# Regrouping SyncE's loads in a fused graph-attention and hypergraph kernel: adjacency ahead of the store, blocks behind the sums' read

## The chip, the cores and the metric

The kernel runs on one core of a Trainium2 chip. The metric is device time in microseconds (us) of one execution; the number quoted for the kernel before is the median of three runs. The profile is one further execution, recorded by the hardware profiler, with a time of its own.

## The reference

The input is a batch of 128 graphs, each with 128 nodes of 512 features (`x`) and a 128 x 128 adjacency (`adj`). Two layers follow each other, both with a residual and a layer norm. Cut to what matters:

```python
# layer 0: graph attention, 8 heads of 64
feats = einsum('bnf,hfu->bhnu', X, W)
dense = leaky_relu(e_self[..., :, None] + e_neigh[..., None, :], 0.2)
att   = softmax(dense - 1e10 * (1 - A), -1)
x = layernorm(x + relu(att @ feats + b))
# layer 1: hypergraph convolution twice, H = (adj != 0), w = first row of adj
conv(x, W) = Dn * (H @ (Be * (H.T @ (x @ W.T)))) + b     # Dn = 1/(H @ w), Be = 1/column sums of H
h = layer_norm(relu(conv(x, W1)))        # 512 -> 1024
x = layernorm(x + (conv(h, W2) + x))     # 1024 -> 512
```

All of it is in float32.

## The kernel before

Two graphs are one **pair**; there are 64 pairs, and everything is done a pair at a time with the 128 nodes on the 128 partitions. The pairs are pipelined: while one pair has its features made, the one before it is in its attention, the one before that in the hidden layer, and a fourth in its output. Matrix products on TensorE (PE) use a scheme with seven half-size products instead of eight, whose sums are made by GpSimd (POOL), whose intermediate copies are made by ScalarE (ACT), and whose last additions are made by VectorE (DVE).

The order of all work is written out by hand. Each step has a due time inside a period of `T = 38.6` units and a lag in periods; the list `todo` is sorted by that time, and the instructions of each engine are issued in the sorted order. The units are those of the schedule, not of the chip. What is due early stands early in its engine's queue, and each engine runs its queue in order. So a due time of a load sets nothing but its place in SyncE's (SP) queue.

SP issues nearly all DMAs, and no other work. In one period it issues, by due time within the period (numbers are line numbers of the profile):

- at 6.2 `e_write` (623): the exponentials of the first half (`nb`) are written to DRAM as `ed`; at 10.0 `e_read` (631) reads them back in four DMAs as `eb`, so that DVE can transpose them blockwise into `eT` (640); at 10.9 and 14.9 the same for the second half;
- at 17.0 `write_nodes` (374): the scales of the nodes, made by DVE in `nodes` (360 to 369) from the adjacency `a` and its first row `w`;
- at 19.5 `store` (1043): the output of a pair that is done;
- at 20.5 `load_edges` (137): the adjacency once more in blocks of 32 x 32, `ab`, in four DMAs, which DVE transposes in `edges` (421);
- at 25.0 `spread_rows` (552), the write of one small tile as `rd`; at 27.0 `neighbours` (570), which reads it back as `nb` for all partitions, 512 KB twice; these are the neighbours' part of the scores. POOL adds the mask to them (589), ACT applies the leaky activation (605) and, in the next period, the exponential (619);
- at 28.0 `spread_nodes` (576, `dnb`); at 28.92 `write_sums` (962, `sd`); at 31.0 `load_rows` (120, `x`); at 31.5 `read_sums` (967, `sums_out`);
- at 0 of the next period `load`: the adjacency `a` (106) and its first row for all partitions, `w` (112), two DMAs;
- at 2.0 `load_blocks` (129): the features in blocks of 32 rows, `xb`, in four DMAs, which DVE transposes in `x_transpose` (385) as input of the feature products.

The tiles of `a` and `w` have two buffers; `xb` and `ab` have one each, so that the load for a pair waits until DVE has transposed the blocks of the pair before. In the program's instruction list, each DMA of SP also waits on the completion of the eighth DMA before it, since eight completion semaphores are used in turn.

ACT's queue matters too: the copies of the propagated features, `zT` (831), which the next hidden products on PE wait for, stand behind the leaky activations of two quarters of the scores.

The last pairs have due times of their own, and so has the start (the dictionary `first`); pairs 0 and 1 load in another order.

Of the kernel before, what the change touches and what calls it, by code (L numbers as in the profile page):

```python
# [20 lines left out]
def kernel(  # L21
# [1102 lines left out]
    for t, fn, *args in (  # L1124
# [14 lines left out]
    T = 38.6  # L1139
    todo = [  # L1140
        (11.1, prepare_first, (0,)), (12.0, prepare_first, (1,)), (15.45, prepare_first_sums, ()),
        (12.1, load_weights, (nc.scalar, w2_blocks, w2t, DH // 2, QU)),
        (13.05, prepare_vectors, ()),
        (14.05, load_weights, (nc.scalar, w1_blocks[:2], w1t, F // 2, HALF)),
        (12.95, load_first_row, (1,)),
        (15.46, load_weights, (nc.sync, w1_blocks[:1:-1], w1t, F // 2, HALF)),
        (16.1, everywhere, (b2_bc, b2, nc.sync)),
        (79.0, prepare_hidden, (nc.gpsimd, 0)), (79.1, prepare_hidden, (nc.gpsimd, 1)),
# [54 lines left out]
        todo.append((time, run, (fn, p, args)))  # L1203
    for p in range(PAIRS):
        if p > 1:
            todo.append(({2: 79.5, 3: 143.1}.get(p, p * T), load, (p,)))
            todo.append((16.2 if p == 2 else p * T + (19.0 if p == 3 else 2.0), load_blocks, (p,)))
            todo.append((p * T + (28.5 if p == 2 else 20.5), load_edges, (p,)))
        for lag, time, name, pairs, fn, args in steps:
            if p not in pairs:  # L1210
                continue
            if p == 0 and lag == 2 and time < 8.5:
                time *= 0.2
            if p == LAST:

                time = {
                    ("attend", 0): 24.25, ("attended", 0): 25.5,
                    ("attend", 1): 25.95, ("attended", 1): 26.0,
                    ("residual", 1): 26.3, ("rstds", "a"): 26.4,
                }.get((name,) + args[:1], time)  # L1220
            if p == LAST - 1:
                time = {
                    ("product", 2): 24.22 if (lag, time) > (3, 20.0) else time,
                    ("product", 5): 29.5 if (lag, time) > (3, 20.0) else time,
                    ("squares", 0): 26.5, ("squares", 1): 26.6, ("h_sums", 2): 22.3,
                    ("h_rstd",): 4.6, ("y_scale", 1): 5.8, ("y_scale", 0): 5.9,
                }.get((name,) + args[:1], time)
            time += (p + lag) * T
            todo.append((
                first.get((name, p) + args, first.get((name, p), time)), run, (fn, p, args)  # L1230
            ))
# [46 lines left out]
```

## Time and profile before

| what | value |
|---|---|
| time, median of 3 runs | 2394.72 us (2393.39 to 2398.32) |
| the profiled execution's own time | 2398.11 us |
| its span, first to last instruction | 2396.3 us |
| TensorE (PE) matmul busy | 2361.6 us, 99% |
| VectorE (DVE) busy | 2087.9 us, 87% |
| GpSimd (POOL) busy | 1823.2 us, 76% |
| ScalarE (ACT) busy | 1528.2 us, 64% |
| SP's DMA queue, share of 16 DMA engines | 50.1% |
| moved | 347.09 MB, mean 145 GB/s |
| granted TensorE clock | 0.997 |

Landing times, median from issue to landing: `nb` 6.0 us for 512 KB, `ed` 3.6 us for 512 KB, `eb` 2.9 us for 128 KB, `x` 4.5 us for 512 KB, the store 2.9 us for 512 KB, `xb` 5.5 us for 128 KB, `a` 2.3 us for 128 KB, `w` 5.1 us for 64 KB, `dnb` 7.8 us for 128 KB, `ab` 2.5 us for 32 KB.

How to read it: a busy time is the time in which an engine had an instruction of its own at work, and PE's is near the whole span. DMA-issuing instructions are not counted as busy; the time in SP's rows is the time that SP needs to issue, and the landing is given apart. The chain of waits is followed back from the end of the program, at each step to what released an instruction or to the one before it on its engine.

### The profile page before, as it was taken

The page shows a single profiled execution, that of the slowest core. Times are in us where ns is not written, and L with a number is a line of the kernel's source. Part 1 is how long each engine was busy: PE and PEld are TensorE (multiplying, and loading weights), DVE is VectorE, ACT ScalarE, POOL GpSimd, SP SyncE. Part 2 cuts the span into 40 slices and gives each one's busy share as a digit, 9 for nine tenths or more (in the row PEclk, how much of TensorE's full clock was granted, in tenths as well). Part 3 has the DMA queues.
Part 4 walks back from the last instruction along what each step waited for, and adds up shares of the span by engine and source line. Part 5 has one row for each costly group of instructions (what it writes and reads, how often), then busy time and mean ns, then how long its engine had stood idle before and what let it go on. Part 6 is the DMA issues. An engine that isn't in the chain of part 4 may idle for free.

```text
span 2396.3 us, 80729 instructions
## 1 busy us (share of the span) xinstructions
PE 2361.6 (99%) x32309; PEld 1898.1 (79%) x32309; DVE 2087.9 (87%) x4456; ACT 1528.2 (64%) x4481; POOL 1823.2 (76%) x2060
## 2 busy tenths in 40 slices
PE   7999999999999999999999999999999999999998
PEld 6777777778778878778778788788888888788886
DVE  7988888888898898898888888988988988988875
ACT  4565765756667667667667566676676675676672
POOL 5877777777777877877877778778778778778774
PEclk9999999999999999999999999999999999999999
DMA  6555555555555555555555555555555555555541
GB/s 197 133 145 153 144 138 142 151 145 148 143 148 147 153 146 150 145 145 153 146 144 156 142 148 151 150 146 146 148 146 152 147 149 141 149 151 144 147 129 37
DMA packets 431134, 347.09 MB, mean 145 GB/s; under 512 B 151440, under 2 KB 380328, under 8 KB 430760
## 3 DMA queue, kind: packets, MB, share of 16 engines
q1 hardware_dynamic: 427288, 337.46, 50.1%
q8 instruction: 256, 4.19, 0.8%
q10 hardware_dynamic: 3472, 4.47, 0.6%
q14 instruction: 118, 0.97, 0.2%
HBM read 239.08 MB, written 102.73 MB: 143 GB/s over the span
## 4 chain that ended last, share of the span: by engine, by line
PE 81%; DMA 8%; DVE 4%; ACT 3%; POOL 2%; SPq 1%; issue 1%; DVEq 0%; POOLq 0%; ACTq 0%
PE phX L97 16%; PE pyX L97 15%; PE pfX L97 8%; PE phW L97 8%; PE pyW L97 7%; PE phY L97 4%; PE pfW L97 4%; PE pav L705 4%; PE pq L97 4%; PE pz L97 4%; PE pyY L97 4%; DMA ed<-nb 3%; DMA nb<-rd 2%; PE pfY L97 2%; ACT nb L605 1%; DMA rd<-rows 1%
## 5 line engine op out<-in xcount | busy, mean ns | idle before, releaser
L344 ACT COPY py<-pyX 128x257 f32<-128x257 f32 x189 | 70.6, 374 | 535.4 <-PE pyX L97 441.2
L97 PEld LDWEIGHTS phX<-zS,w_sb 128*64 128x64 f32 x6144 | 346.2, 137 | 37.8 <-POOL ft L744 23.4
L97 PE MATMUL phX<-zS,w_sb 128*64 128x128 f32 x6144 | 369.0, 273 | 2.6 <-ACT ph L344 2.6
L906 POOL TENSOR_TENSOR sq<-sq 128x512 f32<-128x512 f32 (+2 forms) x384 | 343.1, 894 | 20.1
L589 POOL TENSOR_TENSOR nb<-nb,neg 128x512 f32<-128x512 f32 x256 | 319.7, 1283 | 38.1 <-DMA nb<-rd 22.8
L605 ACT ACTIVATE nb<-nb,ft 128x128 f32<-128x128 f32 x1020 | 325.4, 392 | 21.8 <-POOL nb L589 21.7
L619 ACT ACTIVATE nb<-nb,nm 128x128 f32<-128x128 f32 x1024 | 319.2, 391 | 4.3 <-DVE nm L611 4.0
L769 POOL TENSOR_TENSOR rso<-veo,mhalf 128x2 f32<-128x2 f32 x63 | 44.1, 700 | 337.9 <-DVE veo L767 337.9
L97 PE MATMUL pyX<-w_sb,hS 128*64 128x257 f32 x2016 | 242.4, 381 | 0.0
L883 ACT ACTIVATE h<-h,vecs 128x128 f32<-128x128 f32 x768 | 240.5, 393 | 2.4 <-DVE h L868 1.4
L97 PE MATMUL pyX<-w_sb,h 128*64 128x257 f32 x2016 | 240.8, 379 | 0.5 <-ACT py L344 0.5
L97 PE MATMUL pyW<-w_sb,hS 128*64 128x256 f32 x2016 | 240.3, 379 | 0.1
L611 DVE TENSOR_REDUCE nm<-nb 128x4 f32<-128x512 f32 x256 | 175.3, 685 | 54.9 <-ACT nb L605 50.5
L744 POOL TENSOR_TENSOR ft<-ft,b_bc 128x512 f32<-128x512 f32 x128 | 203.9, 1613 | 6.2 <-ACT ft L533 6.2
L97 PEld LDWEIGHTS pyX<-w_sb,h 128*64 128x64 f32 x2016 | 149.8, 137 | 70.0 <-ACT py L344 0.9
L97 PEld LDWEIGHTS pyW<-w_sb,hS 128*64 128x64 f32 x2016 | 149.8, 137 | 69.2 <-issue 0.7
L97 PEld LDWEIGHTS pyX<-w_sb,hS 128*64 128x64 f32 x2016 | 144.7, 137 | 60.9
L640 DVE STREAM_TRANSPOSE eT<-eb 128x512 f32<-128x512 f32 x252 | 163.7, 686 | 12.0 <-DMA eb<-ed 11.1
L807 DVE SCALAR_TENSOR_TENSOR o<-y,b_bc 128x512 f32<-128x512 f32 x128 | 166.2, 1337 | 0.0
L1008 DVE SCALAR_TENSOR_TENSOR y<-y,rsh,bw_bc 128x512 f32<-128x512 f32 x126 | 150.2, 1230 | 16.3 <-POOL rsh L1004 16.3
L894 ACT ACTIVATE sq<-h 128x512 f32<-128x512 f32 x256 | 160.8, 629 | 2.1
L469 POOL TENSOR_TENSOR hS<-h 128x512 f32<-128x512 f32 x126 | 161.9, 1285 | 0.0
(178 smaller groups left out, 5568.1 us busy)
## 6 DMA issues: line engine op xcount, KB each, us to landing
nb<-rd SPq DMA_DIRECT2D x127, 512.0 KB, 6.0
ed<-nb SPq DMA_DIRECT2D x126, 512.0 KB, 3.6
eb<-ed SPq DMA_DIRECT2D x504, 128.0 KB, 2.9
x<-in_x_dram SPq DMA_DIRECT2D x64, 512.0 KB, 4.5
out_dram<-o SPq DMA_DIRECT2D x63, 512.0 KB, 2.9
xb<-in_x_dram SPq DMA_DIRECT2D x248, 128.0 KB, 5.5
a<-in_adj_dram SPq DMA_DIRECT2D x64, 128.0 KB, 2.3
w<-in_adj_dram SPq DMA_DIRECT2D x128, 64.0 KB, 5.1
```

Of the source, the lines that this page charges most:

```text
L97: nc.tensor.matmul(to[rows], lhs[:, rows], rhs, start=start, stop=stop, skip_group_check=True)
L469: engine.tensor_tensor(t[:, i], in0, in1, op=op)
L589: nc.gpsimd.tensor_tensor(t, t, neg[:, :, None, :].to_broadcast([P, NB, HH, B]), op=ALU.add)
L605: nc.scalar.activation(t, t, AF.Prelu, bias=s["ft"][:, g, h, 0:1], alpha=SLOPE)
L611: nc.vector.tensor_reduce(s["nm"][:, g, hs], scores(p, s, g, hs).rearrange("p b h j -> p h b j"), AX.XY, ALU.max, negate=True,)
L619: nc.scalar.activation(t, t, AF.Exp, bias=s["nm"][:, g, h:h + 1])
L640: nc.vector.transpose(s["eT"][:, g, hs, :].rearrange("p h (b i) -> p h b i", b=NB), s["eb", g][:, :, hs, :].rearrange("p b h j -> p h b j"),)
L744: nc.gpsimd.tensor_tensor(t, t, b0_bc.rearrange("p (h u) -> p h u", h=H), op=ALU.add)
L807: nc.vector.scalar_tensor_tensor(s["o"][:, g, :], s["y"][:, g, :], 2.0, b2_bc, op0=ALU.mult, op1=ALU.add)
L883: nc.scalar.activation(dst[:, k, :], src[:, k, :], AF.Relu, bias=b1_sb[:, c:c + 1])
L894: nc.scalar.activation(s["sq"][:, g, q * KH // 2:(q + 1) * KH // 2, :], hid(s, g, q), AF.Square, scale=DH ** -0.5,)
L906: nc.gpsimd.tensor_tensor(t[:, :n, :], t[:, :n, :], t[:, n:2 * n, :], op=ALU.add)
```

## The change

Three due times are changed, for pairs from 5 on. Pairs 2, 3 and 4 keep theirs, now written as numbers.

```diff
     for p in range(PAIRS):
         if p > 1:
-            todo.append(({2: 79.5, 3: 143.1}.get(p, p * T), load, (p,)))
-            todo.append((16.2 if p == 2 else p * T + (19.0 if p == 3 else 2.0), load_blocks, (p,)))
-            todo.append((p * T + (28.5 if p == 2 else 20.5), load_edges, (p,)))
+            todo.append(({2: 79.5, 3: 143.1, 4: 154.4}.get(p, p * T - 21.5), load, (p,)))
+            todo.append(({2: 16.2, 3: 134.8, 4: 156.4}.get(p, p * T - 3.5), load_blocks, (p,)))
+            todo.append(({2: 105.7, 3: 136.3, 4: 174.9}.get(p, p * T - 2.8), load_edges, (p,)))
```

Within a period, SP's queue becomes, with the moved loads marked: `ed`, `eb`, `ed`, `eb`, `dd` (374), **`a`, `w` of the next pair**, store, `rd`, `nb`, `dnb`, `sd`, `x`, `sums_out`, **`xb`, `ab` of the next pair**. Before, it was: `ed`, `eb`, `ed`, `eb`, `dd`, store, **`ab` of this pair**, `rd`, `nb`, `dnb`, `sd`, `x`, `sums_out`, **`a`, `w`, `xb` of the next pair**. So `a` and `w` are issued 21.5 units earlier, `xb` 5.5 and `ab` 23.3 units earlier than before. The queues of the other engines keep their order, and the bytes moved are the same.

## The prediction

> **What bounds the kernel now.** I read the page's busy times first: TensorE (PE) is busy 2361.6 us of a 2396.3 us span, so all that any change of loads can win is inside the 34.7 us that are left, and most of those lie in the first 140 us and in the last pair. To see where the rest lies I took the start of the residual addition at line 807, which comes once a pair, as a clock: 44 pairs in a row, from 657.10 to 2257.69, follow each other at 36.37 us almost without exception; the 14 pairs before, from 138.68, do not. The busy times of these two stretches:
>
> ```profile
> 138.68:657.10 518.42, 512.42 (x7060) 405.62 (x7058) 451.84 (x967) 333.30 (x981) 396.05 (x449) 1.00 0.52 145
> 657.10:2257.69 1600.59, 1600.48 (x22180) 1294.47 (x22178) 1420.09 (x3037) 1048.11 (x3081) 1249.89 (x1409) 1.00 0.53 148
> ```
>
> The columns are the stretch, its length, and the busy time of PE, weight loads, VectorE (DVE), ScalarE (ACT) and GpSimd (POOL), then clock, DMA share and GB/s. In the second stretch PE is never idle: 1600.59 / 44 = 36.38 us a pair is PE's own time, and no load can shorten it. In the first, 518.42 / 14 = 37.03 us: 14 x 36.38 = 509.3, so 9.1 us are lost there, and they are the whole prize. Later pairs add 0.4 us of it.
>
> PE's waits in the first stretch name the place:
>
> ```profile
> PE phX L97 <- ACT zT L831: 4.7, 7, 1.5
> ```
>
> (A few more end with the transposed attention matrix eT.) ACT is late with zT because its queue holds the leaky activations of the next scores before it. What those wait for is in the chain of waits through this stretch, which PE leaves altogether for two pairs (start, length, what):
>
> ```profile
> 356.50 6.30 DMA ed<-nb
> ...
> 364.67 4.74 DMA ed<-nb
> ...
> 371.01 3.21 DMA eb<-ed
> ...
> 376.33 2.61 DMA rd<-rows
> 378.96 4.69 DMA nb<-rd
> ...
> 393.46 6.66 DMA ed<-nb
> ```
>
> The reader is to see a loop of transfers: exponentials of one half written to DRAM (`ed`, 6.3 us) and read back transposed, the other half likewise, then the small write `rd`, the broadcast `nb`, scores, and again `ed`. It is 393.46 - 356.50 = 36.96 us long, 0.6 more than PE's pair. In these pairs the loop, not PE, sets the time. In the chain of a later pair (1639.9 to 1676) there is nothing but PE.
>
> SyncE's (SP) own order of issues, one pair of the slow stretch, shows what stands next to the two transfers of the loop that can be moved by the change:
>
> ```profile
> 484.51 0.40 SPq L1043 DMA_DIRECT2D out_dram<-o  x1
> 484.96 2.47 SPq L137 DMA_DIRECT2D ab<-in_adj_dram  x4
> 487.53 0.40 SPq L552 DMA_DIRECT2D rd<-rows  x1
> 490.88 0.94 SPq L570 DMA_DIRECT2D nb<-rd  x2
> ...
> 500.51 0.44 SPq L106 DMA_DIRECT2D a<-in_adj_dram  x1
> 500.99 1.39 SPq L112 DMA_DIRECT2D w<-in_adj_dram  x2
> 502.49 1.85 SPq L129 DMA_DIRECT2D xb<-in_x_dram  x4
> 505.71 0.34 SPq L623 DMA_DIRECT2D ed<-nb  x1
> 511.16 1.26 SPq L631 DMA_DIRECT2D eb<-ed  x3
> ```
>
> `nb` is issued as soon as `rd` has landed, `eb` as soon as `ed` has. So `rd` took 3.35 us here, behind the store and four `ab`; in a later pair the same order gives 1654.49 to 1655.99, 1.50 us. And `ed` took 5.45 us, behind `a`, `w`, `xb`; a later pair has 1672.35 to 1674.98, 2.63 us. What flowed meanwhile:
>
> ```profile
> 501.00:505.00 4.00, 3.83 (x72) 3.78 (x72) 2.11 (x5) 4.00 (x14) 3.89 (x8) 1.00 0.21 58
> 505.00:509.00 4.00, 4.00 (x78) 4.00 (x76) 3.52 (x4) 2.92 (x11) 3.78 (x5) 1.00 0.81 251
> ```
>
> While `a` and `w` are at the head (501 to 505) the DMA engines are busy for 0.21 and move 58 GB/s; `xb` and `ed` then crowd into the next four at 251 GB/s. `w` is the row that is read for 128 partitions; the page gives it 5.1 us to land for 64 KB. It holds up what follows.
>
> **What the skill says.** The Trainium skill, DMA: Bandwidth & Descriptors, section "Queues, rings and completion order": each DMA engine consumes one queue's descriptors in ring order. All of SP's transfers are one queue, so a transfer inherits what is ahead of it; 3.35 against 1.50 us for the same 16 KB agrees. The same page, "Why small descriptors are slow (HBM only)": each packet has a fixed overhead. The trace agrees in kind: an `ab` block of 32 KB lands in 2.5 us (median), `a` of 128 KB in 2.3. Perfetto Trace Analysis, "DMA Instruction — HWDGE (DVE, Sync)": SP's time for a DMA does not hold the movement of data; here 0.34 us for `ed` against 2.63 to 5.45 until it has landed. So I count SP's issue time and the landing apart.
>
> **The change, part by part**, per pair from pair 5 on. Nothing is added or removed; eleven DMAs (one `a`, two `w`, four `xb`, four `ab`) change places.
>
> `a` and `w` leave the place ahead of `xb` and go behind the write of the node scales, ahead of the store, a period earlier. At the old place SP gets 500.51 to 502.49 back: 2.0 us. At the new place it spends 0.44 + 1.39 = 1.8 us after 482.73, where in the slow pair it waited for the store's data until 484.51, 1.8 us: hidden, to within some tenths. In later pairs that gap is 1647.33 to 1651.44, 4.1 us. If the cover is gone the store is late, which nothing waits for but its buffer, one period on. Buffers of `a` and `w` are two deep; their last readers, the mask and the node scales two pairs back, are over half a period done, so no wait. The slow `w` now drains ahead of store and `rd`: two `w` issued by 484.6 land 5.1 us later, 489.7, and `rd` must follow.
>
> `ab` leaves the place between store and `rd`: 2.47 us of SP, four transfers of 128-byte runs. `rd` is issued when its rows are ready (SP was late by 0.1 us at most), so the issue wins nothing; the landing does. Bounds for `rd`: it becomes 1.5 us (gain 1.9), or is held by `w` until 489.7 + 0.7 = 490.4 (gain 0.5). I take 1.0.
>
> `xb` moves up by the 2.0 us; `ab` comes behind it, ahead of `ed`. SP: 500.51 + 1.85 + 2.47 + gaps = 505.0, against 505.71 when `ed`'s exponentials are ready: hidden by 0.7 us; beyond it each us of SP delays `ed`, both reads of `eb` and the second `ed` queued behind it. New wait: `ab` has one buffer, so its first block waits for DVE's transpose of the old one (line 421). In the pair at 1200 that ends at 1227.67, and SP gets there after 1232; in a slow one (423.42) it is 3 us ahead too: nothing. Besides, every SP DMA waits for the landing of the eighth before it: `ed` now waits for the first `xb`, 500.5 + 5.5 (median landing) = 506.0, up to 0.3 us late; with `w` gone from its front `xb` should land sooner. Bounds for `ed`: the same load ahead of it and no gain, 0.3 lost; or nothing ahead, 2.63 us, 2.8 gained. With `xb` 2 us earlier and 128 KB of small runs in place of 256 KB with the slow row I take 1.5 gained.
>
> Sum on the loop: -1.0 - 1.5 = -2.5 us (bounds -0.5 + 0.3 = -0.2 to -4.7) against 0.65 needed to get from 37.03 under 36.38. PE binds from then on; what is won beyond that is slack. At the switch pair 5's `a`, `w` still meet pair 4's `ab` ahead of one `rd` (SP's issues at 113.5 to 117.6): up to 1 us once. The loop wins 1.8 us a pair on PE, so some two pairs are needed to catch up: 0.5 to 1 us lost. So 1.7 us of the 9.1 stay, 7.4 go: 2398.11 (the profiled execution; its span is 2396.3) - 7.4 = 2390.7. It was 3.4 us above the median of the runs, 2394.72. PE's part being fixed, I read that as 3.4 us fewer lost in the loop: the median run loses some 9.1 - 3.4 = 5.7 and its floor is 2398.11 - 9.1 = 2389.0, or 2388.6 with the later 0.4. Of 5.7 I leave 1.2: 2390.2 us.
>
> **The rivals.**
>
> *Nothing to see.* The slow stretch ends at 657 by chance (after one PE wait of 1.5 us the loop ran uncongested), and `ab` and `w` only change places as obstacles: -0.2 on the loop. Then the runs spread as before, 2393 to 2397. For it: the bytes per pair are the same. Against: both transfers sit in the chain of waits by name, and 58 GB/s is no saturated engine.
>
> *Slower: `ed` is gated.* Place: SP between the sums' read and the write of `ed`. `ab` behind `xb` takes more than the 0.7 us of cover (one `xb` issue took up to 2.3 us, one `w` 2.0), or the first `xb` lands late. In fast pairs `ed` can land some 2.5 us later before DVE waits (last read of `eb` issued to its transpose 5.5 us, landing 2.9); from there the loop binds in all pairs. At the price of the slow stretch, 0.65 us, 44 more pairs are 29 us: 2423; a third of them gives 2404. For it: in pairs 7 to 9 `ed` takes 5.8 to 6.7 us, eT is late by up to 2.0 and PE by 0.5. Against: the work that is taken from ahead of `ed` is slower than what is put there.
>
> *More than forecast.* The loop is short at once and also the unevenness from 100 to 138 (about 1 us over PE's time) goes: 2388.
>
> **How the numbers follow.** Forecast 0.57, with its own range 2388.8 to 2392; more than forecast 0.10; nothing 0.20; slower 0.13. The line of 0.2%, which is about what a measurement of this kernel can tell from no change, is 4.8 us: 2389.9 and 2399.5. The forecast lies across the first: 0.34 of its 0.57 below, 0.23 above; with the 0.10, faster 0.44. Same is 0.23 + 0.19 = 0.42 (0.01 of the "nothing" case goes to slower), slower 0.14. The range leaves out the slower rival and a thin tail below: 2387.8 to 2398.
>
> **What would show it.** The lines of the loop leave the chain of waits after some 250 us, and PE's wait for zT falls from 4.7 us to under 1.5 in the stretch from 138 to 657. `rd` to `nb` is 1.5 to 2.5 us there, `ed` to `eb` 3 to 4.5. SP's store follows `w` with no long wait. The pair stays 36.37 us later on. Wrong it would be if `ed` goes out well behind its exponentials (SP's wait on ACT for line 623 gone) or lands after over 5 us in the later pairs, or if `rd` behind `w` takes 3 us still.

## The result

The changed kernel takes 2392.21 us (median of 18 runs, 2390.08 to 2394.99) against 2396.05 us of the kernel before on the same chip (18 runs, 2393.39 to 2398.49). The ratio is 0.9985, with a 95% interval of 0.9978 to 0.9991. So a gain of 3.8 us, or 0.15%, is there, inside the 0.2% that was named as the line. In a second set, on another chip, the same kernel had a ratio of 0.9989 (0.9982 to 0.9995).

The profiled execution took 2392.25 us, with a span of 2390.5. The same two stretches as for the kernel before, cut by the start of the residual addition at line 807, in the profile of the changed kernel (stretch, length, busy time of PE, weight loads, VectorE, ScalarE and GpSimd, clock, DMA share, GB/s):

```profile
139.16:652.59 513.43, 510.98 (x7060) 406.16 (x7058) 451.28 (x967) 333.75 (x981) 397.91 (x449) 1.00 0.51 147
689.72:2253.78 1564.06, 1564.06 (x21677) 1313.18 (x21675) 1389.55 (x2969) 1024.68 (x3011) 1222.31 (x1377) 1.00 0.52 148
```

The second stretch holds 43 pairs: 1564.06 / 43 = 36.37 us, PE's own time as before. The first holds 14 pairs and is 513.43 - 14 x 36.37 = 4.25 us too long, where the kernel before lost 9.24 us counted in the same way. PE's waits in this first stretch, after:

```profile
PE phX L97 <- ACT zT L831: 2.1, 4, 1.0
```

4.7 us in seven waits have become 2.1 us in four. The chain of waits of the changed kernel, in the same place as the one shown of before, where it leaves PE (start, length, what):

```profile
373.60 0.25 DVE rows L542
...
373.87 3.49 DMA rd<-rows
...
377.80 8.89 DMA nb<-rd
```

`ed` and `eb` are gone from it. What is left is the branch `rd`, `nb`, mask. SP's queue in one pair of the first stretch:

```profile
478.01 0.43 SPq L106 DMA_DIRECT2D a<-in_adj_dram  x1
478.49 0.94 SPq L112 DMA_DIRECT2D w<-in_adj_dram  x2
480.86 0.40 SPq L1043 DMA_DIRECT2D out_dram<-o  x1
483.93 0.33 SPq L552 DMA_DIRECT2D rd<-rows  x1
486.90 0.92 SPq L570 DMA_DIRECT2D nb<-rd  x2
...
496.81 1.86 SPq L129 DMA_DIRECT2D xb<-in_x_dram  x4
498.77 1.88 SPq L137 DMA_DIRECT2D ab<-in_adj_dram  x4
501.96 0.35 SPq L623 DMA_DIRECT2D ed<-nb  x1
506.63 1.73 SPq L631 DMA_DIRECT2D eb<-ed  x4
```

The order is the one that the change describes. `ed` takes 506.63 - 501.96 = 4.67 us here. But `rd`, with no `ab` ahead of it any more, but `a`, `w` and the store, still takes 2.97 us. That second fact was not forecast, and it is what most of the experiments came to be about.

Four figures from the traces serve from here on. Pairs are counted by the clock at line 807; the `rd` that is issued in a pair's interval belongs to the pair two further on. "ed" is the time from the issue of the first of a pair's two writes `ed` to that of its first read, and "rd" from its issue to that of `nb` (medians). "mask" is the start of POOL's mask (line 589) after the pair's clock at line 807 (mean). "loss" is what the pairs take over 36.37 us. Worked out from the traces, in us:

```
            pairs 2 to 15                  pairs 17 to 59
            ed     rd     mask    loss     ed     rd     mask    loss
before      5.83   2.82   24.48   9.2      3.47   1.52   22.98   0.3
after       4.53   2.99   23.89   4.2      2.69   1.43   22.88   0.1
```

The mask tells most of the loss. In 57 of the pairs 1 to 59 of the kernel before, and in 57 of them in the changed one, a pair is longer than 36.37 us by just what its mask starts later than 23.91 us (to within 0.06 us), and no longer where it starts earlier. Summed over the first 14 pairs the mask is late by 9.0 us before and by 3.5 after; the other 0.8 us after lie in pairs 8 and 9, and their cause was not followed. Of the 0.59 us by which the mask came earlier, 0.49 are that `rd` goes out earlier (on average 15.54 us after the clock before, 15.05 after): with `ed` back sooner, the rows are ready in time. The time of `rd` itself gave nothing (2.85 and 2.87 on average), `nb` 0.12.

The kernel before had two kinds of slow pairs. In pairs 2, 3, 7, 8 and 9 `rd` went out late (15.5 to 16.8 us), so the loop was closed; they lost 4.1 us. In pairs 4, 5, 6, 10, 11, 12 and 15 it went out at 15.1 to 15.2 us, so the loop was open, and the slow `rd` itself made the mask late; they lost 5.1 us.

### The profile page after: what moved, and what is told of

Its sections match the earlier page's. It is cut to its first block, busy times and chain, and to the rows that moved or that the text cites. A ratio compares the mean times of both kernels' runs of the same rounds, so it can differ in the third digit from the quotient of the medians.

```text
span 2390.5 us, 80668 instructions
## 1 busy us (share of the span) xinstructions
PE 2357.9 (99%) x32309; PEld 1947.1 (81%) x32309; DVE 2089.6 (87%) x4456; ACT 1529.1 (64%) x4481; POOL 1826.4 (76%) x2060
## 3 DMA queue, kind: packets, MB, share of 16 engines
q10 hardware_dynamic: 3472, 4.47, 0.6%
## 4 chain that ended last, share of the span: by engine, by line
PE 90%; DMA 3%; DVE 3%; ACT 1%; POOL 1%; issue 1%; SPq 0%; DVEq 0%; POOLq 0%; ACTq 0%
PE phX L97 18%; PE pyX L97 16%; PE pfX L97 9%; PE phW L97 9%; PE pyW L97 8%; PE pfW L97 5%; PE phY L97 4%; PE pq L97 4%; PE pav L705 4%; PE pz L97 4%; PE pyY L97 4%; PE pfY L97 2%; DMA nb<-rd 2%; DMA rd<-rows 1%; PE pd L97 1%; PE pf L523 1%
## 5 line engine op out<-in xcount | busy, mean ns | idle before, releaser
L97 PEld LDWEIGHTS phX<-zS,w_sb 128*64 128x64 f32 x6144 | 347.9, 137 | 38.0 <-POOL ft L744 22.8
L97 PEld LDWEIGHTS pyX<-w_sb,h 128*64 128x64 f32 x2016 | 159.4, 136 | 60.5 <-ACT py L344 0.9
L97 PEld LDWEIGHTS pyW<-w_sb,hS 128*64 128x64 f32 x2016 | 159.3, 136 | 59.3 <-issue 0.9
L97 PEld LDWEIGHTS pyX<-w_sb,hS 128*64 128x64 f32 x2016 | 153.2, 136 | 51.9
```

The costliest lines, as they stand in the source:

```text
L97: nc.tensor.matmul(to[rows], lhs[:, rows], rhs, start=start, stop=stop, skip_group_check=True)
```

## Experiments

Each ratio is against the kernel before, run in the same set on the same chip. Ten of the twelve are edits of the changed kernel; `e9_after_again` is that kernel itself, and `e11_before_35` an edit of the kernel before.

**One part alone.** First only the move of `ab` (`a`, `w` and `xb` at their old due times), then only the move of `a` and `w` (`xb` and `ab` at their old ones):

```diff
# e1_ab_only
-            todo.append(({2: 79.5, 3: 143.1, 4: 154.4}.get(p, p * T - 21.5), load, (p,)))
-            todo.append(({2: 16.2, 3: 134.8, 4: 156.4}.get(p, p * T - 3.5), load_blocks, (p,)))
+            todo.append(({2: 79.5, 3: 143.1, 4: 154.4}.get(p, p * T + 0.0), load, (p,)))
+            todo.append(({2: 16.2, 3: 134.8, 4: 156.4}.get(p, p * T + 2.0), load_blocks, (p,)))
# e2_aw_only
-            todo.append(({2: 16.2, 3: 134.8, 4: 156.4}.get(p, p * T - 3.5), load_blocks, (p,)))
-            todo.append(({2: 105.7, 3: 136.3, 4: 174.9}.get(p, p * T - 2.8), load_edges, (p,)))
+            todo.append(({2: 16.2, 3: 134.8, 4: 156.4}.get(p, p * T + 2.0), load_blocks, (p,)))
+            todo.append(({2: 105.7, 3: 136.3, 4: 174.9}.get(p, p * T + 20.5), load_edges, (p,)))
```

> Only the ab blocks are moved (from between store and rd to behind the sums' read, ahead of a, w and xb); a, w and xb stay where the kernel before has them. Theory (the broadcast row w at the head of the queue holds whatever follows it): the write ed still stands behind w, so it takes 5 us or more in the pairs up to some 500 us, and only rd gets shorter, from about 3 to 1.5 to 2 us there; the time gains under half of what the whole change gained, 2394 to 2396 us. Rival (the ab blocks ahead of rd were the obstacle, a and w are not): as fast as the whole change, about 2392 us, and ed below 4.5 us.

Measured: 2465.59 us, ratio 1.0319 (1.0292 to 1.0346), some 70 us above what was expected. SP's queue in a late pair of this kernel:

```profile
1233.11 0.55 SPq L967 DMA_DIRECT2D sums_out<-sd  x1
1233.76 3.33 SPq L137 DMA_DIRECT2D ab<-in_adj_dram  x4
1237.14 0.45 SPq L106 DMA_DIRECT2D a<-in_adj_dram  x1
1237.63 0.94 SPq L112 DMA_DIRECT2D w<-in_adj_dram  x2
1238.62 1.91 SPq L129 DMA_DIRECT2D xb<-in_x_dram  x4
1240.64 0.38 SPq L623 DMA_DIRECT2D ed<-nb  x1
1246.93 1.73 SPq L631 DMA_DIRECT2D eb<-ed  x4
```

SP needs from 1233.76 to 1240.64 to issue what now stands ahead of `ed`, and then `ed` takes 6.29 us. PE's waits from 700 to 2300 us in this kernel, where the view lists none for the kernel before or the changed one up to their last few pairs:

```profile
PE pav L705 <- DVE eT L640: 14.1, 15, 2.7
PE phX L97 <- ACT zT L831: 12.3, 14, 1.5
```

Over the trace `ed` goes out 1.16 us (pairs 2 to 15) and 0.76 us (17 to 59) after its exponentials (medians), where the kernel before and the changed one have 0.06. From 711.11 to 2322.80 a pair takes 1611.69 / 43 = 37.48 us. That is the rival "`ed` is gated", at 1.1 us a pair in place of the 0.65 that it was priced at.

> Only a and w are moved (ahead of the store); ab stays between store and rd, and xb follows the sums' read since nothing is left ahead of it. Theory: ed takes 2.7 us in the late pairs and 4 to 5 us in the early ones, as with the whole change, because w is gone from its front; rd has w, the store and ab ahead of it and takes 3.5 us or more in the early pairs; time 2392 to 2395 us. Rival (ab is the obstacle): no better than before, 2396 us.

Measured: 2399.77 us, ratio 1.0030 (1.0019 to 1.0041), where 2392 to 2395 us was expected. The trace is that of the slowest of the six runs, 2405.74 us. `ed` has the whole of the gain, 4.47 and 2.69 us. But `a` and `w` now stand ahead of the store and `ab`, and in later pairs `rd` goes out late (mean 15.44 us after the clock, 15.09 in the changed kernel) and takes 2.10 us in place of 1.51 on average. 15 of the 43 later pairs have their mask after 23.96 us.

So neither part gains anything alone: the change is an exchange of places, and each half makes room for the other. Plus 3.2% and plus 0.3% become minus 0.15%.

**Is it `w`?** `w` is one row of 512 bytes read for 128 partitions. The next two kernels read 128 different rows in its place from pair 5 on, the adjacency's own; the bytes are the same. In both, the node scales are thus made without the first row, and their output is not the reference's.

```diff
# e5_w_plain (the changed kernel); e7_ab_only_w_plain (e1_ab_only)
-  nc.sync.dma_start(s["w"][:, g, :], adj[2 * p + g, 0, :].partition_broadcast(P))
+  nc.sync.dma_start(s["w"][:, g, :],
+      adj[2 * p + g, 0, :].partition_broadcast(P) if p < 5 else adj[2 * p + g])
```

> The kernel with only ab moved (2465 us), with w loaded as a plain tile from pair 5 on, same bytes and packets; the node scales come out different. Theory (the slow w ahead of xb and ed is what makes that order lose 70 us): ed falls from 6 to 7.5 us to under 4.5 us, and the time to 2390 to 2405 us. Rival (eleven DMAs ahead of ed are too many for SyncE to issue in time, w's slowness apart: ed goes out 0.5 to 2 us after its exponentials): the time stays above 2430 us.

Measured: 2391.06 us, ratio 0.9993 (0.9985 to 1.0001). The DMA issues of `e1_ab_only` (size, median from issue to landing):

```profile
xb<-in_x_dram SPq DMA_DIRECT2D x248, 128.0 KB, 5.6
...
w<-in_adj_dram SPq DMA_DIRECT2D x128, 64.0 KB, 5.4
```

and the same two of `e7_ab_only_w_plain`:

```profile
xb<-in_x_dram SPq DMA_DIRECT2D x248, 128.0 KB, 3.0
...
w<-in_adj_dram SPq DMA_DIRECT2D x128, 64.0 KB, 2.1
```

The queue is the same one that lost 3.2%. With `w` landing in 2.1 us it loses nothing that can be measured: `ed` takes 4.63 and 3.43 us in place of 7.05 and 6.28. In the first pairs it still goes out 1.05 us after its exponentials, later on 0.06. So what gates `ed` in the later pairs is not the number of transfers ahead of it, nor SP's time to issue them, but the broadcast read of one row.

> The changed kernel with w loaded from pair 5 on as a plain tile (each partition its own row of the adjacency) instead of one row for all partitions: the same bytes, packets, instructions and place in the queue; the node scales come out different. Theory (many reads of one row are what makes w slow): w lands in 2.0 to 2.5 us instead of 4 to 5, the store's landing falls from 3.8 to about 2.9 us, the time is equal or up to 2 us lower, since w is no longer ahead of anything urgent. Rival (w is slow for the number of its packets): nothing changes, w still takes 4 us or more.

Measured: 2388.79 us, ratio 0.9982 (0.9973 to 0.9990). `w` lands in 2.3 us in place of 4.0, but `ed` is 4.54 and `rd` 3.10 us in the first pairs, as with the slow `w`. The changed kernel took 2391.19 us in the same set (`e9_after_again`), 2.4 us more; up to pair 60 the two traces differ by 0.3 us only, so where that comes from is not shown. So `w`, which the prediction feared ahead of `rd`, is not why `rd` stays slow.

**What holds `rd`, then?** Two kernels take the two transfers that stand ahead of it away: `a` and `w` behind the read `dnb` (28.2 in place of 17.1 in the period), or the store behind `nb`.

```diff
# e3_aw_behind_dnb
-            todo.append(({2: 79.5, 3: 143.1, 4: 154.4}.get(p, p * T - 21.5), load, (p,)))
+            todo.append(({2: 79.5, 3: 143.1, 4: 154.4}.get(p, p * T - 10.4), load, (p,)))
# e8_store_behind_nb
-    @step(4, 19.5, until=LAST)
+    @step(4, 27.5, until=LAST)
     def store(p, s):
```

> The whole change, but a and w are issued behind the spread of the node scales (dnb) and ahead of the sums' write, so that neither rd nor ed has them directly ahead. Theory: rd falls to 1.5 to 2 us in all pairs (it was 2.9 to 3.5 in the early pairs with the change), the early pairs lose under 3 us on TensorE, and the time is 2389 to 2391 us. Rival (the store's 512 KB hold rd, not w): rd stays near 3 us in the early pairs, and the time near 2392 us. Against both: w ahead of sd and x makes the sums' read late and moves xb and ab into ed: ed above 5 us and 2394 us or more.

Measured: 2392.01 us, ratio 0.9996 (0.9988 to 1.0004); `rd` 2.94 us in pairs 2 to 15 and 1.43 after. The expected fall of `rd` did not come.

> The whole change, and the output's store is issued behind the broadcast read nb instead of ahead of rd. Theory (after the run with a and w behind dnb, where rd stayed near 3 us: the store's 512 KB hold rd in the early pairs): rd takes 1.4 to 1.6 us in all pairs, TensorE loses under 2 us between 138 and 657 us, and the time is 1 to 3 us below the changed kernel's. Rival (rd is slow in the early pairs because the reads of eb are still under way when it is issued): rd stays above 2.5 us there and the time is the changed kernel's. Against both: the store behind nb delays dnb, sd and x, xb is late, ed takes 4 us or more: slower than the changed kernel by 1 us or more.

Measured: 2389.43 us, ratio 0.9985 (0.9978 to 0.9991); `rd` 3.00 us and 1.43. Here `w` is issued some 5 us ahead of `rd` and the store after it, and neither moves it by a tenth. The time is 1.8 us under that of the changed kernel in the same set, as expected, but `rd` is not why.

**The switch.** The interval from pair 1 to pair 2, in which old and new places meet, took 37.36 us before and 38.11 after. This kernel moves `ab` from pair 4 on, to free `rd` there:

```diff
# e6_ab_from4
-            todo.append(({2: 105.7, 3: 136.3, 4: 174.9}.get(p, p * T - 2.8), load_edges, (p,)))
+            todo.append(({2: 105.7, 3: 136.3}.get(p, p * T - 2.8), load_edges, (p,)))
```

> The whole change, with pair 4's ab moved too, so that no rd has both w and ab ahead of it. Theory: the pair's time from 101 to 139 us (38.1 us with the change, 37.4 before) falls to about 37.3, rd there from 4.0 to about 3; the whole kernel gains 0.5 to 1 us against the change: 2391.4 us. Rival (the wait there has another cause, the start of the pipeline): no difference from 2392.2 us.

Measured: 2391.17 us, ratio 0.9991 (0.9983 to 0.9999). The expectation failed: the interval grew to 39.22 us. PE's waits from 100 to 140 us in this kernel:

```profile
PE pav L705 <- POOL hS L469: 1.3, 1, 1.3
PE phX L97 <- ACT zT L831: 1.1, 1, 1.1
```

The first is new, and late on POOL; its cause was not followed further. In `e3_aw_behind_dnb`, where pair 5's `a` and `w` do not stand ahead of pair 4's `ab` and of `rd`, the interval is 36.70 us.

**The scatter.** The changed kernel, once more and with no edit:

> The changed kernel unaltered, on the same chip and against the same runs of the kernel before as the other three of this set, so that they can be compared. Expected: 0.9985 of the kernel before, as measured; its spread is that of the first 20 pairs.

Measured: 2391.19 us, ratio 0.9989 (0.9982 to 0.9995). `rd` takes 2.94 and 1.43 us, `ed` 4.13 and 2.69, and the first pairs lose 2.7 where the first profile had 4.2. The losses of single profiles have to be held against that.

Another part of the scatter is the granted clock. From the clock of pair 60 to the end PE runs the same 1688 matmuls in both kernels. The stretch in the kernel before, then in the changed one (columns as above; the granted clock is the third number from the end):

```profile
2257.69:2396.30 138.61, 128.95 (x1688) 102.34 (x1684) 99.17 (x200) 70.61 (x203) 81.58 (x95) 0.98 0.29 90
2253.78:2390.50 136.72, 127.05 (x1688) 103.59 (x1684) 99.86 (x200) 70.65 (x203) 82.00 (x95) 0.99 0.28 89
```

In the first of them the granted clock is at half for 3.4 us, with PE at work:

```profile
2345.30:2348.70 3.40, 3.40 (x18) 2.41 (x16) 3.26 (x9) 0.00 (x0) 0.30 (x1) 0.50 0.09 33
```

Eight of the fourteen traces have this dip some 51 us before their end, and the stretch takes 138.2 to 139.7 us in them; in the six others it takes 136.7 to 137.4. The runs without a trace fit: in this set the kernel before took 2392.4 us on average in the 31 runs with a mean granted clock of 0.998, 2394.0 in the 20 with 0.997 and 2395.5 in the 6 with 0.996.

**The fetch of instructions.** In every kernel up to here `rd` took 2.5 to 3.2 us in the first pairs and 1.4 to 1.6 in later ones (medians), whatever stood ahead of it, and the change from one to the other was abrupt: in the changed kernel 3.49 us in pair 12 and 1.42 in pair 13. So a cause outside SP's queue was looked for. The list of DMA queues of the changed kernel (packets, MB, share of the 16 engines):

```profile
q1 hardware_dynamic: 427288, 337.46, 49.2%
q8 instruction: 256, 4.19, 0.7%
```

`q8` carries packets of 16 KB, most of which take 0.9 to 1.5 us each. The Trainium skill, Runtime: NRT & Kernel Launch, section "Instruction fetch mechanics", says that each engine's sequencer fetches its instructions in blocks of 16 KiB, 256 instructions, over a DMA queue of its own. 256 x 256 = 65,536, and the page counts 32309 matmuls and as many weight loads on PE, no other engine over 4481: these are PE's. A pair has some 4 of them, so that their place in the pair drifts slowly. Laid against the clock of line 807, in the changed kernel one of them starts at 15.3 to 16.4 us in the first pairs with a slow `rd`, and at 16.35 us or later where it is fast; `rd` is issued at 15.08 and its packets begin 0.8 us later. (Four later pairs have 2.0 to 2.4 us; in three of them a packet of 8 KB of another instruction queue starts at 15.9 to 16.1.)

To test it, tiny matmuls whose results are never read are put at the start of PE, where it waits for `x` until 8.1 us. They shift PE's stream, and with it every later fetch, against all the rest. The edit with 35 of them; two kernels have 14 and 45, and one adds 35 to the kernel before.

```diff
     def x_transpose_first(p, s):
         s["px"] = [bank(f"px_{p}_{g}") for g in range(2)]
+        for _ in range(35 if p == 0 else 0):
+            nc.tensor.matmul(s["px"][0][:32, :2], ident[:, :32], ident[:, :2], start=True, stop=True)
```

> The changed kernel with 14 tiny matmuls in the same place, 28 instructions or 1.0 us of PE's stream. Theory fetch: the fetches that now go out 16.4 to 17.2 us after the clock of line 807 in pairs 17 on come at 15.4 to 16.2, into the zone of rd: rd of pairs 17 to 59 goes up from 1.43 to over 2.4 us in most pairs, while that of pairs 2 to 12 falls to under 2.2, so that slow and fast pairs change places; the loop still fits into PE's pair in the later ones (slack about 2.5 us), so the time is within 0.15% of the changed kernel's. Theory place: rd 3.0 us in pairs 2 to 12 and 1.43 in pairs 17 to 59, as in the changed kernel.

Measured: 2393.38 us, ratio 1.0002 (0.9994 to 1.0010): 14 matmuls whose results nobody reads left nothing of the gain. The fetch came 1.0 us earlier, and `rd` is now slow up to pair 41 and fast from pair 42 on, but for one pair. SP's queue in these two pairs:

```profile
1577.80 0.33 SPq L554 DMA_DIRECT2D rd<-rows  x1
1581.07 0.92 SPq L572 DMA_DIRECT2D nb<-rd  x2
...
1614.19 0.33 SPq L554 DMA_DIRECT2D rd<-rows  x1
1615.62 1.22 SPq L572 DMA_DIRECT2D nb<-rd  x2
```

3.27 and 1.43 us for the same transfer with the same work ahead of it. The DMA packets in the first of them, for the windows 1578.5 to 1579.0, 1579.0 to 1580.0 and 1580.0 to 1581.0, a packet counted where it starts:

```profile
q1 hardware_dynamic: 135, 0.02, 20.4%
q8 instruction: 1, 0.02, 16.3%
...
DMA packets 0, 0.00 MB, mean 0 GB/s; under 512 B 0, under 2 KB 0, under 8 KB 0
...
q1 hardware_dynamic: 9, 0.00, 1.9%
```

In the second pair, 1614.9 to 1615.4 (the fetch starts at 1615.51):

```profile
q1 hardware_dynamic: 144, 0.02, 21.9%
```

In the slow pair 135 of the 144 packets go out at once. The fetch starts at 1578.72 and takes 1.305 us; the last 8 of 128 bytes and one of 4 start at 1580.01, when it is over. 8 of 128 rows are what one of 16 DMA engines would carry; the trace does not name the engine. In the fast pair all 144 are gone before the fetch begins. The Trainium skill, DMA: Bandwidth & Descriptors, "Queues, rings and completion order", has an engine change between queues at the end of a packet only; with a packet of 16 KB, this trace agrees.

The expectation was met for the later pairs (`rd` 2.63 us, median) and half missed for the first ones: pairs 2 to 5 have some 2.0, but 6 to 12 have 2.3 to 2.7, as their fetches lie at 15.1 to 15.7.

> The changed kernel with 35 tiny matmuls on the identity (32x2, never read) put ahead of PE's first transposes, where PE is idle until x has landed at 8.1 us. Some 70 instructions of PE, 2.5 us of its later stream, at about 28 a us. Theory fetch: rd and ed are slow in a pair when the 16 KB packet that fetches PE's next instructions goes out just ahead of them (15.6 to 16.4 us after the clock of line 807 for rd, 2.9 to 2.3 us before it for ed). The fetches move 2.5 us earlier in every pair, so rd of pairs 2 to 15 falls from 3.0 to under 2.0 us (median, some 1.43), ed of pairs 2 to 15 from 4.2-4.5 to under 3.2; ed of pairs 17 on goes up from 2.7 to over 3.2, as its fetch moves into the zone; the loss from 138 to 657 us is under 2.0 us in place of 2.5 to 4.3, and the time 0 to 2 us under that of the changed kernel. Theory place (rd is slow early on because of the transfers that SP queues ahead of it, or of the loop itself): rd stays at 3.0 and ed at 4.2 to 4.5 in pairs 2 to 15, and nothing changes in pairs 17 on.

Measured: 2389.20 us, ratio 0.9983 (0.9977 to 0.9990). The fetch lies at 12 to 13 us in the first pairs, and `rd` is 1.45 us there, `ed` 2.69, loss 0.00. SP's queue of this kernel, at the place that was shown of the changed one:

```profile
479.16 0.40 SPq L1045 DMA_DIRECT2D out_dram<-o  x1
482.23 0.33 SPq L554 DMA_DIRECT2D rd<-rows  x1
484.89 0.92 SPq L572 DMA_DIRECT2D nb<-rd  x2
...
500.09 0.35 SPq L625 DMA_DIRECT2D ed<-nb  x1
502.77 1.73 SPq L633 DMA_DIRECT2D eb<-ed  x4
```

`ed` is 2.68 us in place of 4.67. `rd`, at 2.66, is the one exception among the first ten pairs: a shorter fetch, of 8 KB on another queue, met it at 16.1. From pair 12 on most fetches lie at 14.5 to 15.7, just ahead of `rd`, which takes 1.83 us in the later pairs; `ed` there goes up to 3.13, short of the 3.2 that was expected, and the later pairs lose 1.5 us.

> The kernel before with the same 35 tiny matmuls at the start of PE, nothing else. Theory fetch: rd of pairs 2 to 15 falls from 2.8 to under 2.0 us, the loop of transfers is 0.8 us or more shorter than 36.96 us and PE binds from some 200 us on without any change of the loads; the loss from 138 to 657 us falls from 9.2 to under 5 us, and the time is 3 to 6 us under that of the kernel before (ratio 0.9975 to 0.9988). Theory place: rd and ed as in the kernel before, loss 6 to 9 us, ratio 0.9995 to 1.0005.

Measured: 2395.41 us, ratio 1.0010 (1.0003 to 1.0017). The time was missed, and not by a little: 2.5 us slower in place of 3 to 6 faster. The account of the fetches holds up to pair 11: `rd` falls to 1.48 us (median of pairs 2 to 15), and the first 14 pairs lose 1.25 us in place of 9.2 although no load was moved. The prediction showed `rd` at 3.35 us behind the store and four `ab`; the same pair here:

```profile
477.51 2.75 SPq L137 DMA_DIRECT2D ab<-in_adj_dram  x4
480.36 0.40 SPq L554 DMA_DIRECT2D rd<-rows  x1
481.90 0.94 SPq L572 DMA_DIRECT2D nb<-rd  x2
```

It takes 1.54 us, with the same transfers ahead of it. But from pair 12 on the fetch lies at about 15, `rd` takes 2.66 us in pairs 17 to 59 and `ed`, with `w` ahead of it, 5.19, and the later pairs lose 4.3. The shift moved the loss from the first stretch to the later one. That is not the whole of the 2.5 us: the profiled execution, 2391.55 us, is among the shortest of this kernel, and its trace lacks the dip of the granted clock 51 us before the end. Of its runs, the 11 with a mean granted clock of 0.997 took 2397.4 us on average, the 9 with 0.998 2393.8; what else its median execution loses is in no trace.

Against `e10_after_35`, with the same 35 matmuls in the same set, this kernel is 6.2 us slower. So the change gains with PE's stream shifted too; its gain does not hang on one place of the fetches.

> The changed kernel with 45 tiny matmuls in place of 35 at the start of PE (still before x has landed). 35 had moved the fetch ahead of rd from 15.8 to 13.0 us after the clock of line 807 in the first pairs and 14 to 14.9, so about 0.08 us a matmul; 45 give some 12.2 us in the first pairs and, as with 35 the later ones lay at 14.9 to 15.5, some 14.1 to 14.8 us there, under the 15.08 at which rd goes out in all pairs. Theory fetch: rd of pairs 2 to 15 stays under 1.6 us (median) and that of pairs 17 to 59 falls from 1.83 to under 1.6; ed of pairs 17 to 59 from 3.13 to under 2.9; the loss of the later pairs falls from 1.5 to under 0.6 us with that of the first pairs under 0.5; time 2387 to 2388.5 us, ratio 0.9973 to 0.9982. Theory place: the gain of 35 matmuls was the scatter of a build; rd is back at 3.0 us in some stretch and the ratio at 0.9985 or above.

Measured: 2389.34 us, ratio 0.9981 (0.9973 to 0.9988). Two stretches of this kernel, as above:

```profile
139.34:648.49 509.15, 509.15 (x7061) 419.14 (x7059) 452.55 (x968) 333.51 (x981) 397.69 (x449) 1.00 0.51 148
684.86:2249.29 1564.43, 1564.26 (x21676) 1305.73 (x21674) 1387.79 (x2968) 1023.85 (x3011) 1222.09 (x1377) 1.00 0.52 148
```

509.15 / 14 and 1564.43 / 43 are 36.37 and 36.38 us: nothing is lost in the first stretch and 0.5 us in the second. `rd` is 1.43 us and then 1.71 (1.6 was expected), `ed` 2.65 and 2.67. The time itself was expected at 2387 to 2388.5. In the profiled execution the interval from pair 1 to 2 has grown to 39.01 us, 2.6 over a pair of PE, with one wait of 2.4 us; part of what the pairs won was lost there.

Against the kernel before, no version's interval lies clear of the changed kernel's: those with 35 and 45 matmuls have the lowest ratios of all that leave nothing out, but overlap with it. Only `e8_store_behind_nb` ran in one set with it, 21 runs each, and is 1.8 us shorter there (95% interval of the difference of medians, by resampling, 0.4 to 2.6 us); which wait that is was not followed.

## Why the prediction was right, and where it was not

**The floor.** 36.38 us a pair of PE, which no load can shorten: right. Even with nothing lost a pair takes 36.37 us.

**`ed`, 1.5 us gained** (bounds 0.3 lost to 2.8 gained): right. It went from 5.83 to 4.53 us, 1.3, and in the second profile to 4.13, 1.7. Its reason, that `w` holds up what follows, is what `e7_ab_only_w_plain` shows. But the 4.5 us that are left in the first pairs are not the queue's: with the fetches moved away (`e10_after_35`) the same order gives 2.69.

**`rd`, 1.0 us gained** (bounds 0.5 to 1.9): wrong, and this is the step that failed. It gained nothing, 2.82 to 2.99 us. The prediction put 3.35 against 1.50 us down to the store and four `ab` ahead of it. What it took as agreement with the order of one queue was a packet of another queue, and as far as the trace tells on one of the same DMA engines. It compared a slow pair with a fast one and did not ask what else differed between them; the same `ab` stood ahead of `rd` in both. By the prediction's own words, `rd` at 3 us would mark it wrong; it had `w` in mind, and `e3_aw_behind_dnb` and `e5_w_plain` show that it is not `w`.

**The loop sets the time of the slow stretch, 9.1 us**: right for 4.1 us of it. In the pairs with the other 5.1 us `rd` went out on time, and the loop was not closed; the two pairs whose chain the prediction showed are of the first kind.

**PE binds from some 250 us on, 1.7 of 9.1 us stay**: half right. The loop through `ed` is open, since `rd` goes out 15.05 us after the clock whatever happened in the pair before. But the branch from `rd` on was still over its cover in 7 of the 14 pairs: at 1.43 us its mask starts at some 22.8 us, so it has 1.1 us to spare up to 23.91, and a fetch that meets `rd` costs 1.5 to 2. So 4.2 us stayed (2.7 in the second profile). PE's wait for `zT` in the stretch fell to 2.1 us, not under 1.5 (0.5 in the second profile). In profiled executions the gain was 2398.11 - 2392.25 = 5.9 us in place of 7.4; but only 3.9 of them were there at the clock of pair 60 (2257.69 and 2253.78), and 1.9 came after it, where the granted clock fell before and not after the change. In medians it was 3.8 us in place of 4.5, in the second set 2.2.

**The switch, up to 1 us once**: within its bound. The interval lost 1.0 us before (37.36) and 1.7 after (38.11), 0.75 more, with `rd` at 3.97 us behind `a`, `w`, the store and `ab`. But it scatters: four more traces with the same order of loads there (`e9`, `e10`, `e12`, `e13`) lost 0.7 to 2.6.

**Costed at nothing**: right. SP's cover of 0.7 us ahead of `ed` was enough, with `ed` out 0.06 us after its exponentials. Its price, when the cover is gone, is what `e1_ab_only` shows. A late store cost nothing, not even 8 units later in `e8_store_behind_nb`, where it takes 5.6 us to land.

**The rivals.** "`ed` is gated" was a real mechanism, kept off only because `a` and `w` leave when `ab` comes; the argument against it, that the work put ahead of `ed` is lighter than what is taken away, is what decided. "Nothing to see" named one thing rightly that the forecast did not take up: the slow stretch ends at 657 us by no cause in the loads. It is where the fetch has drifted past `rd`. "More than forecast" needed the interval from 101 to 139 us to shrink, and it grew.

**The number.** 2390.2 us, with its own range to 2392, against 2392.21, 2.0 us over. Of these, 1.3 are the set's: the kernel before was at 2396.05 in it, and the prediction began from 2394.72. The other 0.7 are gain that did not come, and `rd` is the term that was to bring it. That the sum came so near is in part luck. The prediction took PE's part as fixed and read the 3.4 us between the profiled execution and the median as time lost in the loop; but PE's part is not fixed: of what the two profiles differ by, 1.9 us lie behind the clock of pair 60, where the granted clock fell in one of them.

Open: why `e6_ab_from4` has POOL late near 116 us, why the interval from pair 1 to 2 varies by a microsecond or more between executions, and what makes the granted clock fall 51 us before the end in some of them.

## What to carry to other kernels

When the same transfer takes twice as long in some periods of a loop as in others, look at what differs between those periods before blaming what stands ahead of it in both; lay the packets of all DMA queues, the instruction fetches too, against the loop's clock. Moving loads about in one queue is an exchange: price both halves, as one alone can lose twenty times what the two together win. And a difference of a tenth of a per cent between two unrolled kernels can come from where instruction fetches fall, so shift the stream by a few instructions before putting it down to the edit.

## What the runs showed of the hardware

- A 16 KB packet of PE's instruction fetch that starts between the issue of a small DMA and its last packets delays it: in the changed kernel `rd`, 16 KB, takes 2.9 to 3.5 us in place of 1.43 when the fetch starts 0.5 to 1.3 us after its issue. PE itself did not wait for the fetches: it was busy for all of the 509.15 us of the first stretch of `e13_after_45`. The Trainium skill, Runtime: NRT & Kernel Launch, "Instruction fetch mechanics", calls the cost of crossing a 16 KiB boundary mostly hidden: so it was for PE, not for the transfers beside it.
- 35 tiny matmuls, run while PE waited for `x` anyway, moved a loss of 9.2 us in the first pairs of the kernel before to 1.25, and raised that of the later ones from 0.3 to 4.3.
- The broadcast read of one 512-byte row for 128 partitions, 64 KB, lands in 5.4 us and in 2.1 us if the 128 rows are different ones, and what follows it in the queue waits along: `xb` 5.6 and 3.0 us (`e1_ab_only`, `e7_ab_only_w_plain`).
- Eight of fourteen traces have the granted clock at 0.50 for 3.4 us some 51 us before the end; with it the same 1688 matmuls kept PE busy for 128.95 us (kernel before), without it for 127.05 (changed kernel).
